# A graph network with four residual layers on one core: loads of the preamble in one queue, x^T with two tiles interleaved, and the last two batches as groups of one

## The chip, the cores and the metric

The kernel runs on one core of a Trainium2 chip, in fp32. The metric is the device time of one execution in microseconds, the median over several runs. TensorE (PE) has two rows in a profile: PE for the matmuls and PEld for the loads of the stationary operand. VectorE is DVE, ScalarE is ACT, GpSimd is POOL, SyncE is SP. A "q" behind a name (SPq, ACTq) is that engine's issuing of DMAs.

## The reference

x has 64 batches of 256 nodes by 128 channels; adj is 256 by 256 and shared by all batches. Four layers follow each other, each with a residual and a layer norm:

```python
# layer 0: x and three propagations by A (twice, the same A), one weight for each of the 7
x = layernorm(x + sum_k([x, A x, A^2 x, A^3 x, A x, A^2 x, A^3 x][k] @ W0[:, :, k]))
# layer 1
x = layernorm(x + A @ (x @ W1) + b1)
# layer 2, A normalised by the degrees of A + I
x = layernorm(x + (D (A + I) D x) @ W2.T + b2)
# layer 3: a gated unit, five steps; in_matrix and out_matrix are both A
h = x
for _ in range(5):
    m = A @ h;  av = concat([m, m]);  u3 = h @ U3.T + u3_b
    z = sigmoid(av @ W3.T + w3_b + u3);  r = sigmoid(av @ W4.T + w4_b + u3)
    hv = tanh(av @ W5.T + w5_b + (r * h) @ U5.T + u5_b)
    h = (1 - z) * h + z * hv
x = layernorm(x + h)
```

## The kernel before

The 64 batches are worked on in 32 groups of NB = 2. A group's tile is 128 partitions by 512: two batches of two tiles (T = 2) of 128 nodes, so Q = 4 tiles. Up to ACTIVE = 6 groups are in work at once. `Group.record` writes down all operations of one group; nothing is issued then.

A planner (`Plan.order`, line 75) afterwards sets the order of all instructions. Each operation has an engine, a cost, a lag to its consumers, a rank and the tiles it needs from slots (54 for work tiles, 8 PSUM banks, 9 for x, 16 in DRAM). The planner always places the operation that can start first on its engine; of several, the one of lowest rank. The rank of a group is its number; in the last LEVEL = 6 groups it is 26 plus a tenth per group plus a hundredth per operation already recorded, so that these groups advance side by side, each ten operations behind the one before. On the chip every engine follows that order, with semaphore waits, so a queue such as SP's is in order.

**Preamble** (lines 216 to 342). PE runs WARM = 24 transposes of the identity (`warmed`, line 226). adj is loaded (a_nat), transposed (p_at, aT), squared (p_a2, a2T). The weights of layer 0 (w0_raw) become four sums (w0s, line 263): the identity and W0[0], then W0[k] + W0[k+3] for k = 1 to 3. aTp (line 273) is A^T with its rows permuted, written by four SBUF-to-SBUF DMAs. `load` (line 210) takes the issuing engine: adj, w0_raw and the biases are issued by SP, nine other loads (w1s, b1s, six in `raw`, b2s) by ACT.

**Layer 0** (lines 519 to 561) needs x^T as the stationary operand. For the first HEAD = 2 groups PE transposes x (ptx). For the others DVE transposes 32 by 32 blocks (tx, line 469), SP writes the tile to DRAM (dx), and `brought` (line 474) reads it back with four DMAs, which puts the blocks in place. The node index of that x^T is interleaved over the four tiles: `by_node(xT)[:, q]` takes every fourth element, a step of 16 bytes. A^2 x is computed transposed (pmq, mq). `first` multiplies both by w0s into two PSUM banks, `moved` copies the half that A still has to be applied to (v), `second` applies it and adds it in PSUM, `summed` copies the result (s0). `statistics` and `normalise` are the layer norm: DVE's mean and variance (st, mv, ve), a power on POOL (rs), DVE's scaling (y).

**Layers 1 and 2** propagate (pm, m), multiply by the weight (py) and add y with the bias (yb, on POOL).

**The five steps** (lines 586 to 604) hold h transposed (hT): propagation (pmg, mg), products into pr and ph, the gates r, z and hv on ACT, and rh, d, e, hT on DVE. Between steps `packed` (line 486) brings hT back to node order: DVE's block transpose (th), one write to DRAM (dh), and one read per batch (h). That h has two tiles interleaved (`pair_of`, a step of 8 bytes), which the permuted aTp matches.

**The end.** The last END = 4 groups turn hT by PE (pth), the others by DVE and DRAM (tn, dn, hn). Then the residual, the layer norm, and one output DMA per group.

Line 190 is the helper `mm` that records every matmul, 404 the copies out of PSUM, 508 the gates, 515 DVE's two-operand instructions; groups of instructions are therefore told apart by their tiles.

Of the kernel before, what the change touches and what calls it, by code (L numbers as in the profile page):

```python
# [16 lines left out]
HEAD = 2  # L17
LEVEL = 6
END = 4
STEPS = 5  # L20
WARM = 24
# [4 lines left out]
class Val:  # L26
# [3 lines left out]
    def __init__(self, kind, shape, name):  # L30
        self.kind, self.shape, self.name = kind, shape, name
        self.writer, self.readers, self.users = None, [], []
        self.slot = self.ap = None
# [115 lines left out]
def kernel(  # L149
# [42 lines left out]
    SHAPES = {"bank": [P, 512], "x": [P, 512], "w": [P, 512], "dram": [P, 512], "st": [P, Q * 6], "mv": [P, Q * 2],  # L192
              "ve": [P, Q], "rs": [P, Q]}
    slots = {"bank": BANKS, "x": ACTIVE + 3, "w": 54, "dram": 16, "st": 8, "mv": 8, "ve": 8, "rs": 8}
# [3 lines left out]
    def constant(name, shape):  # L198
        v = Val("const", shape, name)
        v.ap = const.tile(shape, F32, name=name)  # L200
        return v
# [4 lines left out]
    def pre(rank, engine, cost, run, reads=(), writes=()):  # L206
        lag = {"SP": 2300, "ACTq": 2700, "PE": 260, "DVE": 260, "ACT": 130, "POOL": 100}[engine]
        plan.add(engine[:3] if engine == "ACTq" else engine, cost, lag, rank, run, reads, writes)

    def load(rank, engine, name, shape, src):  # L210
        v = constant(name, shape)
        queue = nc.sync if engine == "SP" else nc.scalar
        pre(rank, engine, 450, lambda: queue.dma_start(v.ap, src), [], [v])
        return v
# [18 lines left out]
    a_nat = load(-9, "SP", "a_nat", [P, T, N], adj.rearrange("(t p) m -> p t m", p=P))  # L233
# [13 lines left out]
    pre(-8, "DVE", dve_cost(512), lambda: nc.vector.tensor_copy(flat(aT), p_at.ap), [p_at], [aT])  # L247
# [11 lines left out]
    w0_raw = load(0, "SP", "w0_raw", [P, C, K0], w0)  # L259
# [8 lines left out]
    pre(-7, "DVE", 1300, w0_sums, [w0_raw], [w0s])  # L268

# [35 lines left out]


    w1s = load(0, "ACTq", "w1s", [P, C], w1)
    b1s = load(0.1, "ACTq", "b1s", [P, C], bass.AP(tensor=b1.tensor, offset=b1.offset, ap=[[0, P], [1, C]]))
    raw = {name: load(0.2, "ACTq", f"raw_{name}", [P, src.shape[1]], src)
           for name, src in (("w2", w2), ("w4", w4_w), ("w3", w3_w), ("w5", w5_w), ("u3", u3_w), ("u5", u5_w))}  # L310
    b2s = load(0.2, "ACTq", "b2s", [P, C], bass.AP(tensor=b2.tensor, offset=b2.offset, ap=[[0, P], [1, C]]))
# [33 lines left out]
    def view(ap, g):  # L345
        return ap[g * NB:(g + 1) * NB].rearrange("b (t p) c -> p (b t) c", p=P)

    def nat(v):
        return v.ap.rearrange("p (q c) -> p q c", q=Q)

    def parts(v):
        return v.ap.rearrange("p (t b c) -> p t b c", t=T, b=NB)

    def four(v):
        return v.ap.rearrange("p (b k c) -> p b k c", b=NB, k=2)

    def by_node(v):
        return v.ap.rearrange("p (n q) -> p q n", q=Q)
# [4 lines left out]
    def pair_of(v, q):  # L363
        return v.ap.rearrange("p (b c t) -> p b t c", b=NB, t=T)[:, q // T, q % T, :]

    def plain(v):
        return [v.ap[:, b * N:(b + 1) * N] for b in range(NB)]

    def by_block(v):
        o = v.ap.rearrange("p (k b t i) -> b p t k i", k=4, b=NB, t=T)  # L370
        return [o[b] for b in range(NB)]

    class Group:
        def __init__(self, g):
            self.g, self.first, self.last = g, None, None
            self.gate = self.load_gate = ()
            self.count = 0

        def val(self, kind, name):
            return Val(kind, SHAPES[kind], f"{name}_{self.g}")  # L380

        def add(self, engine, cost, lag, run, reads=(), writes=()):
            after = () if self.first else self.gate
            self.count += 1
            rank = self.g
            if self.g >= G - LEVEL:
                rank = G - LEVEL + (self.g - G + LEVEL) / 10 + self.count / 100
            op = plan.add(engine, cost, lag, rank, run, reads, writes, after)
# [7 lines left out]
        def dve(self, cost, run, reads, writes):  # L396
            return self.add("DVE", cost, 260, run, reads, writes)

        def act(self, run, reads, writes, cost=act_cost(512)):
            return self.add("ACT", cost, 130, run, reads, writes)  # L400
# [6 lines left out]
        def statistics(self, tag, s):  # L407
            st, mv, ve, rs = (self.val(k, k + tag) for k in ("st", "mv", "ve", "rs"))

            def stats():  # L410
                for q in range(Q):
                    nc.vector.bn_stats(st.ap[:, q * 6:(q + 1) * 6], nat(s)[:, q, :])  # L412

            def aggr():
                for q in range(Q):
# [4 lines left out]
            self.dve(775, stats, [s], [st])  # L420
            self.dve(410, aggr, [st], [mv, ve])
            self.add("POOL", 1010, 100,
                     lambda: nc.gpsimd.tensor_tensor(rs.ap, ve.ap, half, op=OP.pow), [ve], [rs])  # L423
            return mv, rs

        def residual(self, tag, ps, resid, left=lambda v: v.ap, right=lambda v: v.ap):
            s = self.val("w", "s" + tag)
            self.dve(dve_cost(512), lambda: nc.vector.tensor_add(right(s), left(ps), right(resid)),  # L428
                     [ps, resid], [s])
            return (s, *self.statistics(tag, s))  # L430

        def normalise(self, tag, s, mv, rs):
            y = self.val("w", "y" + tag)

            def run():
                for q in range(Q):
# [3 lines left out]
            self.dve(1030, run, [s, mv, rs], [y])  # L440
            return y

        def propagate(self, tag, h, aTs, ins=None, outs=None):
# [3 lines left out]
            def run():  # L447
                o, a = (outs or plain)(ps), ins or tile_of
                for b in range(NB):
# [3 lines left out]
            self.pe(pe_cost(N, NB * T), run, [h, aTs], [ps])  # L453
            return self.copied("m" + tag, ps)

        def transposes(self, tag, src):
            ps = self.val("bank", "pt" + tag)

            def run():
                for q in range(Q):  # L460
                    nc.tensor.transpose(ps.ap[:, q * P:(q + 1) * P], src.ap[:, q * P:(q + 1) * P], ident)  # L461

            self.pe(pe_cost(P, Q) / 2, run, [src], [ps])
            return ps

        def turned(self, name, src, ins, outs):

            t, far = self.val("w", "t" + name), self.val("dram", "d" + name)
            self.dve(dve_cost(512), lambda: nc.vector.transpose(t.ap.rearrange(outs, k=4, q=Q),
                                                                src.ap.rearrange(ins, k=4, q=Q)), [src], [t])  # L470
# [198 lines left out]
```

## Time and profile before

| | us |
|---|---|
| median of 3 runs | 1396.2 (1394.82 to 1396.5) |
| the profiled execution's own time | 1396.12 |
| its span, first to last instruction | 1394.3 |
| PE busy | 1374.0 (99% of the span) |
| DVE busy | 972.9 (70%) |
| ACT busy | 508.0 (36%) |
| POOL busy | 230.8 (17%) |
| mean granted TensorE clock | 0.994 |

A row of a group reads: line, engine, operation, output tile <- input tiles, shape, count, then busy time in us and the mean ns of one, then the idle time before them and what ended it. A row of a timeline begins with the start and the length in us; `x8` means that eight instructions are merged in it. An fp32 matmul appears as two MATMUL and two LDWEIGHTS instructions. A row of stretches has the stretch, its length, and the busy time of PE, PEld, DVE, ACT and POOL, then the granted clock, the DMA engines' share and GB/s.

### The profile page before, as it was taken

To read this page: it belongs to the slowest core of one execution; us is meant where nothing else is said; L and a number is where in the kernel's file an instruction comes from. 1 tells how busy PE (TensorE), PEld (TensorE's weight loads), DVE (VectorE), ACT (ScalarE), POOL (GpSimd) and SP (SyncE) were. 2 spreads that over 40 slices of the span, in tenths; PEclk is the share of its full clock that TensorE was granted. 3 is DMA by queue.
4 is the path that set the end of the run, shared out by engine and by line. 5 is a ranking of instruction groups with operands and counts; after the bars stand their busy time and mean duration, and the time that the engine had idled before them with its cause. 6 is when DMAs were issued, how large, how long until landed. Compare 5 with 4: busy or idle time off the path is not lost.

```text
span 1394.3 us, 16512 instructions
## 1 busy us (share of the span) xinstructions
PE 1374.0 (99%) x4998; PEld 926.1 (66%) x4998; DVE 972.9 (70%) x2701; ACT 508.0 (36%) x807; POOL 230.8 (17%) x199
## 2 busy tenths in 40 slices
PE   8999999999999999999999999999999999999995
PEld 7866667667666677666766666676666676765552
DVE  4756676767766777757767677775776778775575
ACT  2233433333334333443333333334334323334442
POOL 1401022202210131201202101111121122220000
PEclk9999999999999999999999999999999999999998
DMA  6022243324233332324323334233333232323231
GB/s 172 31 76 81 79 128 106 114 65 118 91 113 91 98 107 76 111 78 136 102 80 106 94 96 117 81 115 88 107 104 108 76 99 84 113 69 98 85 97 53
DMA packets 255049, 133.95 MB, mean 96 GB/s; under 512 B 146545, under 2 KB 226801, under 8 KB 254961
## 3 DMA queue, kind: packets, MB, share of 16 engines
q1 hardware_dynamic: 253664, 132.12, 32.2%
q8 instruction: 40, 0.66, 0.2%
q10 hardware_dynamic: 1296, 0.79, 0.2%
q14 instruction: 49, 0.39, 0.1%
HBM read 67.05 MB, written 65.54 MB: 95 GB/s over the span
## 4 chain that ended last, share of the span: by engine, by line
PE 95%; DVE 3%; issue 1%; DMA 1%; POOL 0%; ACT 0%; SPq 0%; POOLq 0%; DVEq 0%
PE pr L190 29%; PE pmg L190 19%; PE ph L190 19%; PE py L190 16%; PE pm L190 8%; PE pmq L190 4%; DVE y L437 1%; DMA x<-in_x_dram 1%; DVE st L412 1%; POOL rs L423 0%; DVE e L515 0%; DVE hT L515 0%; DVE s L428 0%; DVE d L515 0%; PE pth L461 0%
## 5 line engine op out<-in xcount | busy, mean ns | idle before, releaser
L190 PE MATMUL pr<-mg,w435u5T 128*128 128x512 f32 x640 | 321.0, 593 | 2.0 <-ACT mg L404 2.0
L423 POOL TENSOR_TENSOR rs<-ve,half 128x4 f32<-128x4 f32 x128 | 134.6, 1053 | 1063.4 <-DVE ve L417 1057.3
L515 DVE TENSOR_TENSOR d<-hv,hT 128x512 f32<-128x512 f32 x160 | 111.3, 696 | 190.2 <-ACT hv L508 189.8
L190 PE MATMUL pmg<-aTp,h 128*128 128x256 f32 x1024 | 241.7, 381 | 0.0
L190 PEld LDWEIGHTS pmg<-aTp,h 128*128 128x128 f32 x1024 | 201.3, 197 | 48.6 <-issue 23.3
L515 DVE TENSOR_TENSOR rh<-r,hT 128x512 f32<-128x512 f32 x160 | 115.0, 719 | 131.4 <-ACT r L508 130.0
L190 PEld LDWEIGHTS pr<-mg,w435u5T 128*128 128x128 f32 x640 | 119.9, 190 | 103.3 <-issue 93.0
L404 ACT COPY mg<-pmg 128x512 f32<-128x512 f32 x160 | 93.8, 586 | 237.0 <-PE pmg L190 223.3
L437 DVE TENSOR_SCALAR y<-s,mv,rs 128x128 f32<-128x128 f32 x512 | 146.9, 351 | 37.2 <-POOL rs L423 36.7
L508 ACT ACTIVATE z<-pr,bsum 128x512 f32<-128x512 f32 x160 | 110.0, 688 | 155.8 <-PE pr L190 141.8
L190 PE MATMUL ph<-rh,w435u5T 128*128 128x512 f32 x320 | 162.0, 593 | 0.3 <-DVE rh L515 0.3
L190 PE MATMUL ph<-mg,w435u5T 128*128 128x512 f32 x320 | 162.3, 592 | 0.0
L190 PE MATMUL pr<-hT,w2u3T 128*128 128x512 f32 x320 | 161.3, 593 | 0.4 <-DVE hT L515 0.4
L508 ACT ACTIVATE r<-pr,bsum 128x512 f32<-128x512 f32 x160 | 110.0, 688 | 136.2 <-PE pr L190 134.0
L508 ACT ACTIVATE hv<-ph,bsum 128x512 f32<-128x512 f32 x160 | 110.0, 687 | 53.8 <-PE ph L190 53.3
L515 DVE TENSOR_TENSOR e<-z,d 128x512 f32<-128x512 f32 x160 | 111.7, 702 | 2.5
L515 DVE TENSOR_TENSOR hT<-hT,e 128x512 f32<-128x512 f32 x160 | 109.3, 687 | 2.7
L412 DVE BATCH_NORM_STATS2 st<-s 128x6 f32<-128x128 f32 x512 | 109.4, 277 | 0.8
L190 PEld LDWEIGHTS ph<-rh,w435u5T 128*128 128x128 f32 x320 | 60.1, 190 | 71.6 <-issue 59.2
L190 PEld LDWEIGHTS ph<-mg,w435u5T 128*128 128x128 f32 x320 | 60.5, 190 | 69.5 <-issue 54.3
L190 PEld LDWEIGHTS pr<-hT,w2u3T 128*128 128x128 f32 x320 | 60.0, 190 | 50.4 <-issue 32.0
L490 DVE STREAM_TRANSPOSE th<-hT 128x512 f32<-128x512 f32 x128 | 90.2, 706 | 1.7
(77 smaller groups left out, 1412.9 us busy)
## 6 DMA issues: line engine op xcount, KB each, us to landing
dh<-th SPq DMA_DIRECT2D x160, 256.0 KB, 2.0
h<-dh SPq DMA_DIRECT2D x256, 128.0 KB, 2.5
x<-in_x_dram SPq DMA_DIRECT2D x32, 256.0 KB, 3.2
hT<-dh SPq DMA_DIRECT2D x128, 64.0 KB, 2.0
out_dram<-y SPq DMA_DIRECT2D x32, 256.0 KB, 2.4
dx<-tx SPq DMA_DIRECT2D x30, 256.0 KB, 2.2
xT<-dx SPq DMA_DIRECT2D x120, 64.0 KB, 2.0
dn<-tn SPq DMA_DIRECT2D x28, 256.0 KB, 2.0
```

Of the source, the lines that this page charges most:

```text
L190: nc.tensor.matmul(o, lhsT, rhs, start=start, stop=stop, skip_group_check=shared)
L404: self.act(lambda: nc.scalar.copy(t.ap, ps.ap), [ps], [t])
L412: nc.vector.bn_stats(st.ap[:, q * 6:(q + 1) * 6], nat(s)[:, q, :])
L423: lambda: nc.gpsimd.tensor_tensor(rs.ap, ve.ap, half, op=OP.pow), [ve], [rs])
L437: nc.vector.tensor_scalar(nat(y)[:, q, :], nat(s)[:, q, :], mv.ap[:, 2 * q:2 * q + 1], rs.ap[:, q:q + 1], op0=OP.subtract, op1=OP.mult)
L490: self.dve(dve_cost(512), lambda: nc.vector.transpose(turn.ap.rearrange("p (u j t) -> p u t j", t=T, j=32), src.ap.rearrange("p (u t i) -> ...
L508: self.act(lambda: nc.scalar.activation(t.ap, ps.ap, func, bias=bias[1], scale=1.0), [ps, bias[0]], [t], act_cost(512) + 100)
L515: self.dve(dve_cost(512), lambda: nc.vector.tensor_tensor(out(t), way(a), way(b), op=op), [a, b], [t])
```

## The change

It has three parts and the generalisation that they need.

- **Preamble.** `load` loses its engine: all loads are issued by SP, ordered by ranks that follow the need (a_nat -9; x of group 0 has 0; w0_raw 0.01; x of group 1 has 1; w1s 1.3, b1s 1.4, the others 1.5). WARM is 12. aT is copied out of PSUM by ACT, not DVE. The planner counts a lag of 4500 ns for the first x loads, 2700 for the others.
- **x^T.** For groups beyond HEAD (now counted in batches: 4) DVE's transpose writes with two tiles interleaved, and one DMA per batch reads the tile back from DRAM, with 256-byte pieces. Channels come out permuted: partition 4j + r holds channel 32r + j. A second copy of the first two weight sums, w0p, has its rows permuted to match; four SBUF-to-SBUF DMAs on SP make it.
- **Groups of one.** A group has its own nb, start and width; `ONES = (0, 2)` makes the last two batches groups of one, so that there are 31 groups of two and two of one. Their tiles use half of a slot. END is counted in batches (8). The gates that limit the groups in work count batches. x loads take the group's rank, which matters in the last region.

```diff
-WARM = 24
+WARM = 12
+ONES = (0, 2)
...
-    def load(rank, engine, name, shape, src):
+    def load(rank, name, shape, src):
         v = constant(name, shape)
-        queue = nc.sync if engine == "SP" else nc.scalar
-        pre(rank, engine, 450, lambda: queue.dma_start(v.ap, src), [], [v])
+        pre(rank, "SP", 450, lambda: nc.sync.dma_start(v.ap, src), [], [v])
...
-    pre(-8, "DVE", dve_cost(512), lambda: nc.vector.tensor_copy(flat(aT), p_at.ap), [p_at], [aT])
+    pre(-8, "ACT", act_cost(512), lambda: nc.scalar.copy(flat(aT), p_at.ap), [p_at], [aT])
...
-    w0_raw = load(0, "SP", "w0_raw", [P, C, K0], w0)
+    w0_raw = load(0.01, "w0_raw", [P, C, K0], w0)
...
+    w0p = constant("w0p", [P, 2, C])
+
+    def permuted():
+        for r in range(4):
+            nc.sync.dma_start(w0p.ap.rearrange("(j r) k c -> r j k c", r=4)[r], w0s.ap[32 * r:32 * (r + 1), 0:2, :])
+
+    pre(1.2, "SP", 1800, permuted, [w0s], [w0p])
...
+        def rank(self):
+            g = self.start / NB
+            return g if g < G - LEVEL else G - LEVEL + (g - G + LEVEL) / 10 + self.count / 100
...
-            plan.add("SP", 450, 2700, g, lambda: nc.sync.dma_start(nat(x_), view(x, g)), [], [x_],
+            plan.add("SP", 450, 4500 if self.start < HEAD else 2700, self.rank(), lambda: nc.sync.dma_start(nat(x_), self.view(x)), [], [x_],
                      self.load_gate)
 
-            if g < HEAD:
-                xT = self.copied("xT", self.transposes("x", x_))
+            near = self.start < HEAD
+            if near:
+                xT, w01 = self.copied("xT", self.transposes("x", x_)), w0s
             else:
 
-                xT = self.brought("xT", self.turned("x", x_, "p (q k j) -> p q k j", "p (k i q) -> p q k i"))
+                w01 = w0p
+                turn, far = self.val("w", "tx"), self.val("dram", "dx")
+                xT = self.val("w", "xT")
+                self.dve(lambda: nc.vector.transpose(
+                    turn.ap.rearrange("p (r b i t) -> p r b t i", r=4, t=T, i=32),
+                    x_.ap.rearrange("p (b t r j) -> p r b t j", r=4, t=T, j=32)), [x_], [turn])
+                self.add("SP", 420, 2000, lambda: nc.sync.dma_start(far.ap, turn.ap), [turn], [far])
+
+                def run():
+                    f = far.ap.rearrange("(k j) (r b n) -> b (j r) k n", k=4, r=4, b=self.nb)
+                    for b in range(self.nb):
+                        nc.sync.dma_start(xT.ap.rearrange("p (b k n) -> b p k n", b=self.nb, k=4)[b], f[b])
+
+                self.add("SP", 450 * self.nb, 2300, run, [far], [xT])
...
-                    for b in range(NB):
-                        o, n0 = p.ap[:, b * 2 * C:(b + 1) * 2 * C], b * N + t * P
-                        mm(o, xT.ap[:, n0:n0 + P] if g < HEAD else by_node(xT)[:, b * T + t, :], w0s.ap[:, 0:2, :], b == 0, True, shared=True)
-                        mm(o, qT.ap[:, n0:n0 + P], w0s.ap[:, 2:4, :], False, True, shared=True)
+                    for b in range(self.nb):
+                        o, q = p.ap[:, b * 2 * C:(b + 1) * 2 * C], b * T + t
+                        mm(o, (tile_of if near else pair_of)(xT, q), w01.ap[:, 0:2, :], b == 0, True, shared=True)
+                        mm(o, tile_of(qT, q), w0s.ap[:, 2:4, :], False, True, shared=True)
...
+    sizes = [1] * ONES[0] + [NB] * ((B - sum(ONES)) // NB) + [1] * ONES[1]
     groups = []
-    for g in range(G):
-        group = Group(g)
-        if g >= ACTIVE:
-            group.gate = (groups[g - ACTIVE].last,)
-        if g >= ACTIVE + 2:
-            group.load_gate = (groups[g - ACTIVE - 2].last,)
-        elif g >= HEAD:
-            group.load_gate = (groups[g - HEAD].first,)
+    for i, nb in enumerate(sizes):
+        group = Group(sum(sizes[:i]), nb)
+        end = group.start + nb
+        done = [o for o in groups if o.start + o.nb <= end - NB * ACTIVE]
+        loaded = [o for o in groups if o.start + o.nb <= end - NB * (ACTIVE + 2)]
+        if done:
+            group.gate = (done[-1].last,)
+        if loaded:
+            group.load_gate = (loaded[-1].last,)
+        elif group.start >= HEAD:
+            group.load_gate = (groups[i - 2].first,)
```

The rest of the diff replaces NB, Q and the fixed widths by the group's own, in shapes, loops and planner costs.

## The prediction, made before the change was run

> **What bounds the kernel now.** I read the page's busy shares first, then the busy time of three stretches, then the timelines of the two ends, then the groups by shape. Page:
>
> ```profile
> span 1394.3 us, 16512 instructions
> PE 1374.0 (99%) x4998; PEld 926.1 (66%) x4998; DVE 972.9 (70%) x2701; ACT 508.0 (36%) x807; POOL 230.8 (17%) x199
> PE   8999999999999999999999999999999999999995
> ```
>
> Stretches (PE busy is the third figure):
>
> ```profile
> 0.00:18.67 18.67, 14.73 (x70) 12.98 (x71) 7.69 (x21) 4.50 (x8) 1.42 (x7) 0.91 0.53 154
> 18.67:1355.00 1336.33, 1335.43 (x4861) 900.58 (x4860) 941.74 (x2609) 494.14 (x785) 225.34 (x188) 1.00 0.33 97
> 1355.00:1394.30 39.30, 23.80 (x69) 12.52 (x67) 23.49 (x74) 9.32 (x14) 4.03 (x4) 0.84 0.19 54
> ```
>
> PE idles 0.9 us in 1336: the middle is PE work laid end to end, and only less PE time per group shortens it. The ends are latency. The head, from chain, timeline and 2-us stretches (last three figures: granted clock, DMA share, GB/s):
>
> ```profile
> 1.36 5.19 PE L228 MATMUL warm<-ident 128*128 128x128 f32 x24 [1.36 <-POOL ident masks.py:199]
> 2.21 8.02 DMA x<-in_x_dram
> 11.39 2.61 PE p_a L190 x8
> 14.67 1.99 PE pmq L190 x8
> ...
> 8.00:10.00 2.00, 0.73 (x4) 0.42 (x4) 1.59 (x7) 0.00 (x0) 0.00 (x0) 0.91 0.62 184
> 10.00:12.00 2.00, 1.72 (x6) 1.58 (x7) 0.70 (x3) 0.89 (x2) 0.00 (x0) 0.50 0.36 81
> ```
>
> The adjacency lands at 3.73, but its transposes wait until 6.28 behind 24 warm-up transposes; then PE, in order, waits for x of groups 0 and 1 (landed at 9.2 and 10.2, 7.4 and 8.0 us after issue; the median of this load is 3.2), and squares A at a granted clock of 0.50. Dense work, from py of group 0, starts at 18.8.
>
> The tail:
>
> ```profile
> 1371.29 0.69 ACT L508 ACTIVATE hv<-ph,bsum 128x512 f32<-128x512 f32 x1 [0.17 <-PE ph L190]
> 1374.77 3.44 PE L190 MATMUL pmg<-aTp,h 128*128 128x256 f32 x8
> 1384.97 0.69 DVE L515 TENSOR_TENSOR hT<-hT,e 128x512 f32<-128x512 f32 x1
> 1390.14 1.12 DVE L437 TENSOR_SCALAR y<-s,mv,rs 128x128 f32<-128x128 f32 x4 [1.19 <-POOL rs L423]
> ```
>
> From 1374.7 one group of two batches goes down a chain that nothing fills, its pmg at half clock (3.44 where 1.89 is usual). By shape:
>
> ```profile
> L190 PE MATMUL py<-w0s,xT 128*128 128x256 f32 x256 | 80.8, 397 | 0.0
> L190 PE MATMUL py<-w0s,mq 128*128 128x256 f32 x256 | 76.1, 379 | 0.0
> L190 PEld LDWEIGHTS py<-w0s,xT 128*128 128x128 f32 x256 | 69.6, 309 | 9.3 <-issue 2.6 <-PE py L190 0.7 <-PE pr L190 0.5
> L190 PEld LDWEIGHTS pmg<-aTp,h 128*128 128x128 f32 x1024 | 201.3, 197 | 48.6 <-issue 23.3 <-PE ph L190 4.1 <-PE pr L190 2.6
> ```
>
> x^T with four tiles interleaved (16-byte steps) takes 309 ns to load as weights; h, with two interleaved, takes 197 and is hidden.
>
> **Part 1, x^T.** Eight py instructions (four on xT, four on mq) take 1.79 us at 32.27 and at 35.06, and 1.72 in group 0, where xT is contiguous: 0.07 per half group, 0.14 per group. The new layout has h's step, and pmg on h goes at the pace of pmg on y (241.7/1024 and 60.5/256, both 236 ns), so all of it goes: 30 groups' worth x 0.14 = **-4.2 us**, on PE's path in the packed middle. Beside it: DVE's transpose falls from 1110 ns (row tx) to about 706 (th), 12 us in all, costing nothing on a 70% DVE; SP issues two loads a group for four (60 issues fewer at 0.45-0.6), into twice as many 256-byte pieces, landing as h does in 2.5 us for 2.0. SP and DMA (share 0.33) are covered as long as xT arrives before PE reaches it. w0p adds four SP issues (part 2) and a wait of PE's: py of group 2 wants it, issued by about 11.6 and landed, at aTp's 3.4, by 15, far ahead of 26.
>
> **Part 2, the preamble.** All loads go to SP: a_nat, x0, w0_raw, x1, then nine that ACT issued (9 x 0.45 = 4.1 us of SP time), then aTp (four issues, 2.44 us before), w0p (four, taken the same, also bounded by h's 0.47 each: 1.9 to 2.4), x2, and the biases (six, 4.9 us before). SP thus reaches aTp near 6.7, x2 near 11.7 (11.97 before), dx of group 2 near 17 (17.69 before). The xT loads of group 2 then land near 22.5; PE needs them at 32.27 before, 26.4 after an advance of 5.9. So nothing is cost for SP's extra work, with some 4 us of cover; What stands behind w0p's wait for w0s in SP's queue is x2, the biases and dx2; w0s follows w0_raw (6.5 before) by some 1.5 us of DVE, so SP, there at 9.2, doesn't wait. aTp and the step weights are needed much later. ACT, freed, copies aT (586 ns by the a2T row, 692 on DVE).
>
> x0: 512 KB stand ahead of its end instead of most of the 1.8 MB moved by 10 us. At the 400 GB/s seen near 3 us it lands by 4.5; with the dip to 100 GB/s at 4.3-5.3, by 6. PE doesn't want it before 7.5. The Trainium skill (DMA: Bandwidth & Descriptors, "Issuing engines are not separate DMA queues") says queues share the same 16 DMA engines, so a second queue only saves issue time. Alone, that gives no gain here and 4.1 us more of SP; the row of 8.0 against 3.2 says order matters. I take the row; by the rule alone x0 would stay at 9.2 and the head gain fall to about 4.
>
> PE: 12 warm-ups at 0.21 end near 3.9; p_at four at half clock 0.86, to 4.8; aT copy to 5.4; p_a2; a2T copy; ptx0, ptx1 beside it; pmq0, pmq1 (1.73 each), p_an and the two weight transposes (1.1 together). If the clock rises at 6.2 as in this trace: p_a2 ends at 7.5, pmq0 starts at 8.4, dense work 8.4 + 3.45 + 1.1 = 12.95, a gain of 5.9. The clock is the doubt. The trace: warm-ups 206 ns apart (p_an's, at full clock: 140 to load), so half clock until about 6.2; falls at 9.6, rises at 13.0. The skill (TensorE: Matmul & The Clock Gate, "The HAM clock gate") wants about 3.4 us of sustained activity in a free-running window; 12 warm-ups give 2.6, and PE then idles 0.65 for aT. By the rule p_a2 may stay at half until 9.6: it ends at 8.9, dense work starts at 14.85, a gain of 4.0. The trace's window of 9.6-13.0 was about 89% busy and did raise the clock; the new one would be near 79%. I take between, leaning to the trace: **-5.3 us** (ends -2.5, with x late too, and -7).
>
> **Part 3, two groups of one.** Before, from 1355 PE has 20.7 us of work at full clock in 39.3: 18.6 lost. Of this 14.0 lie after the last pmg starts at 1374.66 (19.64 less 5.6 of work), the rest are waits of 0.67, 0.68 and 3.05 and small ones. With one batch the same chain is: pmg four at 0.215 and 0.17 to read, 1.03; copy 0.43; pr 0.6; r 0.47 (688 less 256 columns at 0.83); rh 0.42 (the 256-wide DVE copy: 411); ph 0.6; hv 0.47; d, e, hT 1.26; pth 0.35; s 0.42; st, mv, ve 0.85; rs 1.05; y 0.6; output 3.05 as before. Sum 11.6, with 3.3 of PE work: 8.3 lost. Before it stands the round trip of h (th, dh, h: 6.6 us before, about 5.9 with one load), filled by the other single, five operations ahead, and the last pair; I leave 2 us of gaps and 0.5 of half clock. Lost 10.8, a gain of 7.8. Costs: `second` streams 128 columns, 1.08 per batch by the py<-w1s row against 1.72 per pair, +0.45; more short DVE and ACT instructions and two more chains of POOL powers (1.05 each; POOL 17%) lie beside PE; seven groups stand open in the last region where six did, on 54 slots and 8 banks. No row shows that: from 0 (PE loses 0.9 us in the middle now) to the whole gain; I take 0, since singles hold a bank half as long. The new ranks of x loads only bring late x forward, at no cost with nine x slots. Net **-7.3 us** (-3 to -9.5).
>
> **Sum.** -4.2 - 5.3 - 7.3 = -16.8 on the profiled run's own 1396.12 (span 1394.3 and 1.8 around it), 0.1 from the median of 1396.2: **1379.3 us**. About 0.2% (2.8 us) is what a measurement of this kernel can tell from no change.
>
> **Rivals.**
> - *The head hardly pays* (0.16): half clock until 9.6 and PE empty near 25, as xT of group 2 comes late. For: SP has 13 issues ahead of everything. Against: freed ACT, the cover above. 4.2 + 7.3 + 1.5: about 1383.
> - *The tail hardly pays* (0.15): fixed latencies (rs 1.05, output 3.05, DMA round trips near 6) don't halve, and two singles in step wait at the same times, PE idling before each pmg. For: the 3.05 idle of before is just such a round trip. Gain 2 instead of 7.3: 1384.6; with the head at its low end of 2.5 as well, 1387.4.
> - *x^T stays slow, or PE's pace isn't set by those loads*: the change doing not what it says (0.03): 1383.5.
> - *Slower* (0.04): SP's single in-order queue becomes the bound at the start. If one of its waits (w0p on w0s, dx2 on DVE) holds x2, dx2 and xT behind it, PE has only groups 0 and 1 to work on. It decides once xT of group 2 lands later than 26.4 plus the gain, near 43; at 48 the run is 1401. Against: w0_raw stands third in the queue and landed at 6.5 even in the crowd.
>
> **How the numbers follow.** The forecast's own case has 0.62 and spans 1375 to 1383.5. The rivals of 1383 to 1387 have 0.34 together; a range of 1374 to 1387 leaves out the slower case, mixtures of two weak parts, and a tail or head better than both ends. Faster by over 0.2%: 0.94; within: 0.02; slower: 0.04.
>
> **What would show it.** py<-xT weight loads near 197 ns with matmuls at 379; tx near 0.7 us; x0 landed by 6 and py of group 0 starting near 13 (14.9: the clock rule was right); PE unbroken from there to some 20 us before the end; last pmg about 11.6 us before the end. Wrong: idle PE between 20 and 60 us or in the last 170, py of group 0 after 16, or a last pmg over 15 us before the end.

## The result, and the profile after

The changed kernel takes 1383.24 us (median of 6 runs, 1381.69 to 1384.2), the kernel before 1395.4 in the same comparison (6 runs, 1394.66 to 1396.5): a ratio of 0.9911 with a 95% interval of [0.9899, 0.9924], 12 us less. The profiled execution took 1382.45, with a span of 1380.7. A second set of runs of the same kernel gave 1381.79 (after2, below); the experiments are set against that one. The kernel before varies with its mean granted clock: over the 38 executions run beside the experiments its span goes from 1390.1 us at a clock of 0.998 to 1394.9 at 0.994, while the changed kernel's eleven lie between 1379.6 and 1382.4 at 0.997 or 0.998, so at a like clock the difference is nearer to 10 us than to 12.

The page's head, after. PE busy fell by 7.5 us; the last of the 40 slices went from 5 to 6 tenths, the first from 8 to 9.

```profile
span 1380.7 us, 16602 instructions
PE 1366.5 (99%) x5044; PEld 922.5 (67%) x5044; DVE 970.5 (70%) x2735; ACT 513.1 (37%) x833; POOL 236.1 (17%) x205
PE   9999999999999999999999999999999999999996
```

Three stretches (first the length, then the busy time of PE, PEld, DVE, ACT and POOL; last three figures: clock, DMA share, GB/s). The packed middle loses 1.0 us in 1325, as it lost 0.9 in 1336 before.

```profile
0.00:14.52 14.52, 12.48 (x54) 10.79 (x55) 5.33 (x17) 4.59 (x8) 1.42 (x7) 1.00 0.56 165
14.52:1340.00 1325.48, 1324.47 (x4880) 892.54 (x4879) 934.31 (x2620) 494.42 (x798) 229.90 (x193) 1.00 0.34 97
1340.00:1380.70 40.70, 29.55 (x113) 19.16 (x111) 30.85 (x99) 14.11 (x27) 4.83 (x6) 0.94 0.25 68
```

The groups by shape, after: the load of x^T as weights takes 196 ns where it took 309, the matmul 379 where it took 397 (means).

```profile
L195 PE MATMUL py<-w0p,xT 128*128 128x256 f32 x240 | 71.5, 379 | 0.0
L195 PEld LDWEIGHTS py<-w0p,xT 128*128 128x128 f32 x240 | 46.2, 196 | 14.8 <-issue 9.4 <-PE py L195 0.7 <-PE pr L195 0.5
```

The head, from PE's timeline. Names are shown without their numbers, so p_a is the squaring of A (p_a2 in the kernel and in the expectations). Read the second column: p_a takes 3.78 us, twice the 1.89 of pmq, which has as many instructions of the same shape. And the last line has no bracket: PE comes to pm of group 0, the first matmul of layer 1, without an idle gap.

```profile
5.71 3.78 PE L195 MATMUL p_a<-aT,a_nat 128*128 128x256 f32 x8 [0.68 <-ACT aT L251]
9.29 1.50 PE L475 MATMUL ptx<-ident,x 128*128 128x128 f32 x8
11.06 1.89 PE L195 MATMUL pmq<-a2T,x 128*128 128x256 f32 x8
27.26 1.89 PE L195 MATMUL pm<-aT,y 128*128 128x256 f32 x8
```

The same matmul in the kernel before:

```profile
30.76 1.89 PE L190 MATMUL pm<-aT,y 128*128 128x256 f32 x8
```

x of groups 0 and 1 lands 3.6 and 4.7 us after its issue, where it took 7.4 and 8.0.

The tail. The first four lines are PE's timeline, from the last batch's last pmg on; the others are DVE's in the same stretch, where instructions of three groups alternate (128x512 is pair 60, 128x256 are the batches 62 and 63). PE waits 2.64 us for an hT of DVE, and DVE has no gap over 0.6 us between 1367 and 1376.

```profile
1367.27 1.03 PE L195 MATMUL pmg<-aTp,h 128*128 128x256 f32 x4
1368.75 0.70 PE L195 MATMUL pr<-mg,w435u5T 128*128 128x256 f32 x2 [0.46 <-ACT mg L419]
1370.77 0.60 PE L195 MATMUL ph<-rh,w435u5T 128*128 128x256 f32 x2
1374.00 0.41 PE L475 MATMUL pth<-ident,hT 128*128 128x128 f32 x2 [2.64 <-DVE hT L529]
```

```profile
1369.80 0.42 DVE L529 TENSOR_TENSOR hT<-hT,e 128x256 f32<-128x256 f32 x1
1370.15 0.42 DVE L529 TENSOR_TENSOR rh<-r,hT 128x256 f32<-128x256 f32 x1
1370.67 1.11 DVE L451 TENSOR_SCALAR y<-s,mv,rs 128x128 f32<-128x128 f32 x4
1371.70 0.42 DVE L443 TENSOR_TENSOR s<-pth,y 128x256 f32<-128x256 f32 x1
1372.04 0.41 DVE L529 TENSOR_TENSOR d<-hv,hT 128x256 f32<-128x256 f32 x1
1372.37 0.48 DVE L427 BATCH_NORM_STATS2 st<-s 128x6 f32<-128x128 f32 x2
...
1377.08 0.60 DVE L451 TENSOR_SCALAR y<-s,mv,rs 128x128 f32<-128x128 f32 x2 [0.88 <-POOL rs L438]
```

By place: the matmuls on x^T give 4.5 us (busy time of their rows: 80.8 before; 71.5 and, for the first two groups, 4.8 after). Pm of group 0 starts at 27.26 for 30.76: 3.5 from the head. The rest of the 13.6 between the spans, about 5.6, is the tail's, with whatever the groups of one cost elsewhere; in after2, whose span is 1380.0, the same remainder is 6.3.

### The profile page after: what moved, and what is told of

Same layout as the page of the kernel before. It is cut to its first block, busy times and chain, and to the rows that moved or that the text cites. A ratio compares the mean times of both kernels' runs of the same rounds, so it can differ in the third digit from the quotient of the medians.

```text
span 1380.7 us, 16602 instructions
## 1 busy us (share of the span) xinstructions
PE 1366.5 (99%) x5044; PEld 922.5 (67%) x5044; DVE 970.5 (70%) x2735; ACT 513.1 (37%) x833; POOL 236.1 (17%) x205
## 4 chain that ended last, share of the span: by engine, by line
PE 97%; DVE 2%; DMA 0%; ACT 0%; issue 0%; POOL 0%; SPq 0%; POOLq 0%; DVEq 0%
PE pr L195 30%; PE ph L195 19%; PE pmg L195 19%; PE py L195 16%; PE pm L195 8%; PE pmq L195 4%; DVE y L451 1%; DMA h<-dh 0%; DVE st L427 0%; PE p_a L195 0%; PE warm L232 0%; DVE s L443 0%; DVE d L529 0%; DVE mv L431 0%; DVE e L529 0%
## 5 line engine op out<-in xcount | busy, mean ns | idle before, releaser
L195 PE MATMUL pr<-mg,w435u5T 128*128 128x512 f32 (+1 forms) x660 | 323.3, 580 | 1.7 <-ACT mg L419 1.4
L438 POOL TENSOR_TENSOR rs<-ve,half 128x4 f32<-128x4 f32 (+1 forms) x132 | 137.9, 1049 | 1049.8 <-DVE ve L432 1049.7
L529 DVE TENSOR_TENSOR d<-hv,hT 128x512 f32<-128x512 f32 (+1 forms) x165 | 113.6, 690 | 189.6 <-ACT hv L522 189.2
L529 DVE TENSOR_TENSOR rh<-r,hT 128x512 f32<-128x512 f32 (+1 forms) x165 | 116.5, 706 | 128.2 <-ACT r L522 126.9
L195 PE MATMUL pr<-hT,w2u3T 128*128 128x512 f32 (+1 forms) x330 | 163.1, 580 | 1.1 <-DVE hT L529 1.1
L522 ACT ACTIVATE z<-pr,bsum 128x512 f32<-128x512 f32 (+1 forms) x165 | 111.3, 674 | 142.2 <-PE pr L195 137.4
L195 PE MATMUL ph<-mg,w435u5T 128*128 128x512 f32 (+1 forms) x330 | 163.4, 579 | 0.0
L195 PE MATMUL ph<-rh,w435u5T 128*128 128x512 f32 (+1 forms) x330 | 163.0, 579 | 0.0
L529 DVE TENSOR_TENSOR e<-z,d 128x512 f32<-128x512 f32 (+1 forms) x165 | 113.8, 691 | 2.5
L529 DVE TENSOR_TENSOR hT<-hT,e 128x512 f32<-128x512 f32 (+1 forms) x165 | 113.1, 687 | 2.5
```

The lines of the kernel that those rows point to most:

```text
L195: nc.tensor.matmul(o, lhsT, rhs, start=start, stop=stop, skip_group_check=shared)
L438: lambda: nc.gpsimd.tensor_tensor(rs.ap, ve.ap, half[:, :self.q], op=OP.pow), [ve], [rs])
L522: self.act(lambda: nc.scalar.activation(t.ap, ps.ap, func, bias=bias[1], scale=1.0), [ps, bias[0]], [t], act_cost(self.width) + 100)
L529: self.dve(lambda: nc.vector.tensor_tensor(out(t), way(a), way(b), op=op), [a, b], [t])
```

## The experiments

Twelve runs follow, one of them the changed kernel again. Each ran beside the kernel before on the same chip, and the ratios are to it. Here x is late or early by the time from its issue to its landing, and "pm of group 0" is the first matmul of layer 1.

**Undoing the two parts that can be undone alone.**

```diff
 # ones00
-ONES = (0, 2)
+ONES = (0, 0)
 # oldxt
-                w01 = w0p
...
+                w01 = w0s
+                xT = self.brought("xT", self.turned("x", x_, "p (q k j) -> p q k j", "p (k i q) -> p q k i"))
```

> The changed kernel with the last two batches again as one group of two (ONES = (0, 0)); preamble and x^T stay new. If the singles are worth what is left of the profiled gain after the head (3.7) and x^T (4.3), 13.6 - 8.0 = 5.6, this run is 5 to 6 us slower than the changed kernel, near 1388.5, and its last pmg starts 18 to 20 us before the end. If the tail gained from the clock or the order and not from the width, the run is within 2 us of the changed kernel.

> The changed kernel with the old x^T (four tiles interleaved, four reads of 64 KB per group, weights w0s); w0p is still written, but nothing reads it. If the 16-byte step of the weight load is what cost PE 0.14 us per group, loads of py<-w0s,xT take about 309 ns again, matmuls 397, and the run is 4.0 to 4.7 us slower than the changed kernel, near 1387.5. If the PE's pace was not set by those loads, it is within 1 us.

ones00: 1387.48 (1385.6 to 1389.66), ratio 0.9957 [0.9945, 0.9969], 5.7 over after2. From the last pmg to the end its profiled execution takes 17.6 us where the changed kernel takes 13.4:

```profile
1366.23 1.90 PE L195 MATMUL pmg<-aTp,h 128*128 128x256 f32 x8
```

This last pmg ran at full clock, where the kernel before, in the same order and behind the same wait of 3.05 us, had taken 3.44. So of the 19.5 of before, 2.0 were half clock in the tail of that one execution and 4.2 the size of the group. The profiled execution is the fastest of ones00's six, whose spans go from 1383.8 at a mean clock of 0.998 to 1387.9 at 0.995. So 4.2 of the 5.7 is shown as the width of the group; that the rest is the clock is likely, but none of the longer executions was traced.

oldxt: 1386.47 (1386.33 to 1388.21), ratio 0.9946 [0.9935, 0.9958], 4.7 over after2. Its weight loads are slow again:

```profile
L195 PEld LDWEIGHTS py<-w0s,xT 128*128 128x128 f32 x256 | 69.2, 305 | 11.0 <-issue 4.1 <-PE pr L195 1.0 <-PE py L195 0.2
```

So x^T is worth what the changed kernel's own trace gave it (4.5), and the tail about as much (5.6). In both runs something else was seen that neither touches: p_a took 1.99 us and not 3.78, from the same start in ones00 and from 5.49 in oldxt, and PE then waited before pm of group 0. This is ones00:

```profile
5.71 1.99 PE L195 MATMUL p_a<-aT,a_nat 128*128 128x256 f32 x8 [0.68 <-ACT aT L251]
26.91 1.97 PE L195 MATMUL pm<-aT,y 128*128 128x256 f32 x8 [1.21 <-DVE y L451]
```

The head of ones00 is the changed kernel's, instruction by instruction, and p_a begins at 5.71 in both. So p_a's pace was not set by the head's order.

**PE's wait ahead of p_a, filled.** Four identity transposes fill PE's wait for aT.

```diff
 # fill4
+    def filled():
+        for i in range(FILL):
+            nc.tensor.transpose(warm.ap[:, (i % 4) * P:(i % 4 + 1) * P], ident, ident)
+
+    pre(-8, "PE", 700, filled, [p_at], [warm])
```

> The changed kernel with four more identity transposes on PE between p_at and p_a2, where PE waits 0.7 us for aT. If the idle gap (and so a window that is not busy enough) kept the clock at half through p_a2, the clock now rises near 6.2, p_a2 takes about 2.2 us instead of 3.8, py of group 0 starts near 13 instead of 14.5, and the run is 1 to 1.8 us faster, near 1381.7. If the clock's rise follows the start of the warm-up by a fixed time or the gap does not matter, p_a2 stays at 3.8 and nothing moves (within 0.3).

fill4: 1381.92 (4 runs, 1381.89 to 1382.13), ratio 0.9912 [0.9899, 0.9925]: no less than the changed kernel (0.9911 and 0.9916), though p_a took 1.99 us and py of group 0 started 1.9 us earlier. That the filling brought the clock isn't shown: p_a took 1.99 in unfilled kernels too, and 2.69 in s0first, which has the same filling. PE's line and DVE's timeline of fill4 show where the 1.9 went:

```profile
27.27 1.97 PE L196 MATMUL pm<-aT,y 128*128 128x256 f32 x8 [1.71 <-DVE y L457]
```

```profile
20.74 0.39 DVE L589 COPY s<-py 128x256 f32<-128x256 f32 x1
23.37 0.71 DVE L551 STREAM_TRANSPOSE tx<-x 128x512 f32<-128x512 f32 x1 [2.24 <-DMA x<-in_x_dram]
24.00 0.39 DVE L589 COPY s<-py 128x256 f32<-128x256 f32 x1
24.31 0.85 DVE L433 BATCH_NORM_STATS2 st<-s 128x6 f32<-128x128 f32 x4
...
26.78 1.12 DVE L457 TENSOR_SCALAR y<-s,mv,rs 128x128 f32<-128x128 f32 x4 [0.51 <-POOL rs L444]
```

DVE takes its instructions in order. Between the two copies of group 0's s0 stands the block transpose of a later group, whose x SP issued late (near 18 us in the changed kernel, behind everything else in its queue); it waits 2.24 us, and group 0's layer norm waits with it. Pm of group 0 starts at 27.27, 0.01 from the changed kernel's. The same came out in warm24, which undoes the shorter warm-up:

```diff
-WARM = 12
+WARM = 24
```

> The changed kernel with 24 warm-up transposes again in place of 12. Theory (the warm-up is beside the wait for adj and p_a2's clock decides nothing, as pm of group 0 waits for y): warm-up ends by 5.0, p_a2 starts at most 1.2 later than in the changed kernel if all 24 run at half clock and not later if they run at full clock, first pm of group 0 between 26.9 and 27.6, time within 0.7 of the changed kernel's 1381.8. Rival (a longer warm-up brings the full clock earlier and that is worth its 1.9 us): p_a2 at 2.0 us instead of 3.8, first pm of group 0 near 25.5, time about 1380. Rival (12 more transposes hold up p_at): p_at starts after 4.8 instead of 3.76, all later work 1 us later, time about 1382.8.

warm24: 1382.6 (4 runs, 1382.3 to 1382.89), ratio 0.9914 [0.99, 0.9928]. The warm-up held p_at up to 5.79, p_a started at 7.06 and ran in 1.99 us; PE waited 0.98 us for y and started pm of group 0 at 27.55. The theory's time (within 0.7) was missed by 0.1, and the rival's 1380 did not come. The other rival was right that p_at is held up, and near in time (1382.8); but pm of group 0 came only 0.3 later for it, and the intervals can't tell the cost from none.

**Clearing what stands ahead of group 0's layer norm**, in two ways: x of groups 2 and 3 earlier and the biases later (early12); then, on top of fill4, DVE's order itself (s0first).

```diff
 # early12
-    pre(2.5, "SP", 2200, biases, [], [braw])
+    pre(5.5, "SP", 2200, biases, [], [braw])
...
-        elif group.start >= HEAD:
+        elif group.start >= 2 * HEAD:
 # s0first, in Group.record of fill4
+                if self.start >= 2 * HEAD:
+                    self.gate = (*self.gate, held[0])
...
             y = self.normalise("0", s0, *self.statistics("0", s0))
+            if self.start == 0:
+                held.append(self.last)
+                plan.add("DVE", 150, 150, 0.4, lambda: nc.vector.tensor_add(bsum.ap, braw.ap[:, :3], braw.ap[:, 3:]),
+                         [braw], [bsum], (self.last,))
```

(early12 also ranks the x loads of groups 2 and 3 at 1.45 and 1.46.)

> The changed kernel with x of groups 2 and 3 loaded without a gate and ahead of the step weights in SP's queue, and the six bias loads moved behind (rank 5.5). If what sets the head is SP's one queue (x of groups 2 to 4 late, DVE holding its transposes in order ahead of the first layer norm's copy, and PE waiting for y), the copy s of group 0 comes right after `second`, y of group 0 lands near 23.5 to 24.5 instead of 26.5 and the run is 1 to 2.5 us faster than the changed kernel. If the head is set by the clock or by the norm's own latency, it is the same within 0.5.

> The changed kernel with fill4's four identity transposes ahead of p_a2, and with VectorE's order in the head altered: the stream transposes of groups 4 and later, and bsum, come only after y of group 0, so that nothing that waits for a late x or a late bias stands ahead of group 0's second s0 copy. Theory (group 0's first pm waits for y because VectorE takes its instructions in order, 1.71 us in fill4, 1.2 in early12): the first pm of group 0 starts near 25.6 with a wait under 0.3, no other wait of more than 0.5 follows before 45 us, and the time is 1.3 to 1.9 below the changed kernel's 1381.8: about 1380.2. Rival (the gain is given back again by something later, the xT of groups 4 and 6 above all, which are now loaded later): pm1 of group 0 at 25.6, but one or two new waits of PE of together 1.2 to 1.7 between 30 and 50 us; time 1381.5 to 1382. Rival (it is p_a2's clock alone that sets y): pm1 of group 0 still at 27.2; time 1381.9.

early12: 1382.16 (4 runs, 1380.87 to 1382.73), ratio 0.9916 [0.9902, 0.993]. The wait only moved: DVE stood 4.59 and 1.09 us before the transposes of the next groups and 0.53 before bsum, the s0 copies came at 23.57, and PE waited 1.22 before pm of group 0 at 27.20. s0first did clear it, and so shows that DVE's order was the cause of the wait: pm of group 0 starts at 25.92, with none.

```profile
25.92 1.89 PE L196 MATMUL pm<-aT,y 128*128 128x256 f32 x8
```

Yet it took 1381.68 (4 runs, 1381.07 to 1382.09), ratio 0.9907 [0.9894, 0.9921], which the changed kernel's 1381.79 can't be told from. The planner's order differs from there on; PE's waits between 1000 and 1340 us have one that the changed kernel lacks:

```profile
PE ph L196 <- DVE rh L535: 0.8, 1, 0.8
```

From pm of group 0 to the last pmg it needs 1340.7 us, after2 1339.3: the 1.4 of the head is given back, 0.8 of it in that one wait. The other 0.6 I could not place. The gains that were expected of early12 (1 to 2.5) and of s0first (1.3 to 1.9) both failed to come. The rival of a gain given back was right, but not in its place (30 to 50 us) or its cause (a late xT).

**The queue.** The nine loads go to ACT again, first with the aT copy left on ACT (actq), then with it on DVE as before (actq_dve), then also with the lag that the planner assumed for them before, 2.7 us (actq2; in the other two it was 0.13).

```diff
-    def load(rank, name, shape, src):
+    def load(rank, name, shape, src, engine="SP"):
...
+        plan.add(engine, 450, 2300 if engine == "SP" else 2700, rank, lambda: queue.dma_start(v.ap, src), [], [v])
...
-    pre(-8, "ACT", act_cost(512), lambda: nc.scalar.copy(flat(aT), p_at.ap), [p_at], [aT])
+    pre(-8, "DVE", dve_cost(512), lambda: nc.vector.tensor_copy(flat(aT), p_at.ap), [p_at], [aT])
```

> The changed kernel with the nine loads of w1s, b1s, raw and b2s issued by ACT again; the order on SP stays (a_nat, x0, w0_raw, x1). If sharing the DMA engines with a second queue is what made x land 7.4 to 8.0 us after issue, x0 or x1 lands after 7.5 again; PE asks for x only near 9 because of the slow p_a2, so the time moves by 0 to +1 us. If only the place behind w0_raw mattered, x0 lands by 5 and the time is the same within 0.3; aTp and w0p leave SP some 3 us earlier without any effect.

> As in the run with ACT issuing nine loads, but the copy of aT is DVE's again, as before the change, so it isn't caught behind ACT's blocked issue (there aT waited until 10.2). x0 and x1 should land 7 to 8 us after issue again, at 8.5 to 11. If that lateness is what one queue removes, py of group 0 starts 1 to 2.5 us later than in the changed kernel (15 to 16.5) and the time is 0 to 1.5 us longer; if PE has slack for late x (p_a2 runs first), py starts within 0.5 us and the time is the same.

> The changed kernel with the nine loads of w1s, b1s, the raw weights and b2s issued by ACT again as in the kernel before, the aT copy on VectorE, and the planner told the same lag for these loads as before (2.7 us). It parts the queue from the moved copy and from the order of the transposes, which actq and actq_dve mixed in. Theory (two queues put bytes beside x, and x comes later; the single queue is what brings x early): x0 and x1 land 6.5 to 8 us after their issue, PE waits 1.5 to 3 us for x of group 0 ahead of its transposes, first py near 16 to 17.5, and the time is 1 to 2.5 above the changed kernel's: 1382.8 to 1384.3. Rival (the order of the queue costs nothing, as y of group 0 is set by the late loads on SP, which are freed here): x2 and x3 are issued about 4 us earlier, y of group 0 is ready by 26, and the time is 1380.5 to 1381.8.

| | time, us | ratio to before | x lands after its issue | pm of group 0 |
|---|---|---|---|---|
| changed kernel (after2) | 1381.79 | 0.9916 [0.9903, 0.993] | 3.4 and 5.8 | 27.29 |
| actq | 1386.58 | 0.9947 [0.9935, 0.9958] | 7.3 and 8.7 | 32.51 |
| actq_dve | 1389.29 | 0.9965 [0.9953, 0.9978] | 6.5 to 7.9 | 33.30 |
| actq2 | 1385.99 | 0.9938 [0.9924, 0.9951] | 6.0 and 7.3 | 31.82 |

All three are slower than the changed kernel by 4.2 us or more: more than the head had gained. The expectations of actq (0 to 1) and actq_dve (0 to 1.5) missed by far; none of the three had ACT's wait. actq_dve is not a clean reading, since the false lag put two weight transposes ahead of p_a and PE waited 4.21 and 1.95 us there for raw weights; actq2 is cleaner. There the cause is less the late x (PE's transposes of x start at 8.22 with no wait) than ACT itself. ACT's own timeline in actq2:

```profile
2.29 6.53 ACTq L218 DMA_DIRECT2D raw_w<-in_L_gnn_w_w_dram  x3
8.87 1.10 ACTq L218 DMA_DIRECT2D raw_u<-in_L_gnn_u_w_dram  x2
10.01 0.45 ACTq L218 DMA_DIRECT2D b2s<-in_L_gnn_b_dram  x1
10.49 0.59 ACT L261 COPY a2T<-p_a 128x512 f32<-128x512 f32 x1 [8.26 <-DMA raw_w<-in_L_gnn_w_w_dram]
```

The second column of the first line is not issuing time: each of the three issues takes 0.33 to 0.45. It is a wait. A completion semaphore is a counter that a DMA raises when it has landed. The built program of actq2 hands eight of them to its DMAs in turn, whichever engine issues them, and has the issuing engine wait until the last user of the semaphore has landed. The third of the raw_w loads shares its semaphore with w_raw (the profile's name for w0_raw), 448 KB, and so ACT stands until w_raw has landed at 8.47, and the copy of A^2 behind it until 10.49, though PE had ended p_a at 8.4. The chain of waits of actq says it in one line each; there it is aT that stands behind the load, and PE waits 5.79 us for it:

```profile
1.74 8.06 DMA w_raw<-in_L_gnn_weight_dram
9.82 0.34 ACTq L218
10.19 0.59 ACT aT L252
10.83 2.50 PE p_a L195 x5
```

In the changed kernel such waits stop SP alone, for 0.6 us on w_raw and 0.4 on x, and no wait of PE follows from them. And y of group 0 is held in actq2 by the same DVE order as in fill4, later still:

```profile
28.25 0.71 DVE L546 STREAM_TRANSPOSE tx<-x 128x512 f32<-128x512 f32 x1 [3.59 <-DMA x<-in_x_dram]
28.89 0.83 DVE L428 BATCH_NORM_STATS2 st<-s 128x6 f32<-128x128 f32 x4
```

My theory for actq2 had the sign right and the size and place wrong (py of group 0 at 16.88, as it said, but through PE's waits of 1.27 for aT, 1.26 for ahat and 1.09 for a weight, not for x); the rival, that freeing SP would bring x of groups 2 and 3 sooner, fell: SP issued them at 16.16. It had waited 4.5 us, on x's semaphore, before its fifth issue. No run has a late x alone, so what the early x is worth by itself stays open.

**The same kernel again, and the tail.** noln leaves out the last layer norm of pair 60 and of batch 62; ypool keeps it and puts its final multiply on POOL.

```diff
 # noln
-            return (s, *self.statistics(tag, s))
+            return (s,) if tag == "3" and self.start in (60, 62) else (s, *self.statistics(tag, s))
 # ypool, in normalise
+            if tag == "3" and self.start in (60, 62):
...
+                self.add("POOL", 350 * self.q, 100, run_pool, [s, mv, rs], [y])
+                return y
```

> The changed kernel itself once more, to stand beside the other runs of this chip. The squaring of A (p_a2) took 3.8 us in its first profile and 2.0 in profiles of other versions with the same first 8 us, so the phase of the clock's window should be chance: p_a2 can take either 2.0 or 3.8 here. If py of group 0 starts near 12.8 (p_a2 fast), PE will wait 1.2 to 1.7 us for y of group 0 near 26 and the total stays within 0.5 us of the first runs; if the head's gain were set by the clock, a fast p_a2 would give a run 1.8 us faster.

> The changed kernel without the last layer norm of the last pair and of the first single (batches 60, 61 and 62 are written before that norm): 2.5 and 1.4 us of DVE work fewer in the last 15 us; the last single is whole. If DVE's in-order queue lengthens the last chain (13.4 us from the last pmg where 11.6 was worked out for a free DVE), the last pmg now starts 11.3 to 12 us before the end and the run is 1.3 to 2.5 us faster. If the chain's own latencies are longer than worked out, it gains under 0.5.

> The changed kernel with the normalising multiply (y) of the last layer norm of pair 60 and of batch 62 on GpSimd (POOL) instead of VectorE; all else as it is, so the whole result is computed. Theory (the last batch's chain waits in VectorE's queue behind the other groups' norms, 1.1 us by noln, of which the y of pair 60 and of 62, 1.11 and 0.59 us long in the changed kernel, are the larger part): from the last pmg to the end 12.5 to 13.0 instead of 13.4, time 0.3 to 0.8 below the changed kernel's 1381.8. Rival (POOL has no room: it also computes rs, 0.74 and 0.70 us, and the y of 60 and 62 hold up rs of 63): rs of 63 starts over 0.3 after its ve, last pmg to end 13.4 to 15, time 1381.8 to 1383.5.

after2: 1381.79 (1381.33 to 1383.34), ratio 0.9916 [0.9903, 0.993]; pm of group 0 at 27.29, 13.4 us from the last pmg to the end. noln: 1381.11 (1380.77 to 1381.43), ratio 0.991 [0.9896, 0.9923]; 12.3 from the last pmg to the end. DVE's queueing behind the other groups' norms is worth 1.1 us in the trace, 0.7 by the medians, where 1.3 to 2.5 had been expected. ypool could not have it: 1382.59 (1382.0 to 1382.81), ratio 0.9913 [0.9899, 0.9926], 13.6 from the last pmg to the end. POOL's timeline says why, and the rival had it: the four multiplies take 3.39 us there and 1.11 on DVE, and rs of the last batch (last line), whose ve started at 1375.25 and takes 0.17, starts at 1376.12, once POOL is free.

```profile
1370.41 3.39 POOL L457 TENSOR_SCALAR y<-s,mv,rs 128x128 f32<-128x128 f32 x4
1373.77 0.71 POOL L438 TENSOR_TENSOR rs<-ve,half 128x2 f32<-128x2 f32 x1
1374.59 1.57 POOL L457 TENSOR_SCALAR y<-s,mv,rs 128x128 f32<-128x128 f32 x2
1376.12 0.72 POOL L438 TENSOR_TENSOR rs<-ve,half 128x2 f32<-128x2 f32 x1
```

No version that computes everything beats the changed kernel by more than the runs spread: fill4, early12, warm24, s0first and ypool lie between 1381.68 and 1382.6.

## Why the prediction was right, and where its sizes were off

- **x^T: right in mechanism and size.** -4.2 forecast, -4.5 measured in PE's rows, 4.7 when undone. The loads are at h's pace, the transpose at 0.70 us, and xT's two longer loads cost nothing on SP.
- **The order of the loads: right as to x.** It landed at 4.9 and 7.0 (3.6 and 4.7 after issues at 1.24 and 2.28), and PE did not wait for it. The row was taken against the rule of "Issuing engines are not separate DMA queues" (the Trainium skill, DMA: Bandwidth & Descriptors), which left 4 us of head gain for a late x. On the rule's own point, that engines share the DMA hardware, nothing here speaks against it. What decides in actq2 is which engine stands in the wait for a semaphore: ACT, with copies that PE wants behind it.
- **The head: -5.3 forecast, -3.5 measured.** The step that failed is "dense work 12.95, a gain of 5.9", shaded to 5.3 for the clock: it took the start of py of group 0 for the whole gain. Two limits stand at nearly the same time. In the profiled execution p_a ran at half pace and py started at 14.7, the value that the prediction had worked out by the clock rule (14.85, a gain of 4.0). In ones00, oldxt, fill4, early12, warm24 and ypool p_a ran in 1.99 us, py started up to 2.1 earlier, and PE waited 1.0 to 1.7 us before pm of group 0, which starts between 26.9 and 27.6 in all of them. The cover was named for xT of group 2 alone; the wait that was missed is that for y of group 0, in DVE's order behind the transposes of x tiles that the single queue issues last. The first rival's "PE empty near 25" was that wait in place, with another cause. What the 3.5 consists of was not taken apart: in warm24, where p_a ran in 1.99 us, the longer warm-up cost 0.3 before pm of group 0, and the new order of PE's first operations, the early x and the freed ACT were not tried one by one.
- **The tail: -7.3 forecast, about -5.6 measured (6.3 in after2).** Two terms were mis-sized. The chain of one batch was 11.6 by the sum of its own latencies and is 13.4 in the trace. Of the 1.8, noln shows 1.1 to be DVE's queue: with two singles and a pair ending together, DVE is busy 1.82 to 1.93 of each 2 us from 1368 to 1374, and the last batch's d, e and hT take their turns. "More short DVE instructions lie beside PE" was the cost set to nothing that did cost. The remaining 0.7 was not taken apart. And the loss before was put too high: the 69 PE instructions from 1355 on, "20.7 us of work at full clock", are 21.8 us busy in ones00, which ran them at full clock, so 17.5 us were lost and not 18.6 (after the change 11.2, 40.70 less 29.55, for 10.8). The gaps and half clock that it allowed for ahead of the last chain, 2.5, were 1.6, which hid part of this. Of what was gained, 2.0 is half clock that the profiled execution of the kernel before had in its tail and ones00's had not; how often the changed kernel's tail meets it isn't shown.
- **Slot pressure and SP's queue: rightly at nothing.** The middle idles 1.0 us, as before, and no wait for xT appears. The slower rival found nothing to stand on; group 2's xT was issued from 21.3 on and took 2.8 to 3.9 us, and PE wanted it at 28.99; that was later than worked out (SP came to x of group 2 at 13.23 for 11.7), but still in time.

The sum: -4.5 - 3.5 - 5.6 for -4.2 - 5.3 - 7.3, 13.6 for 16.8. The measured 1383.24 is 3.9 above the forecast and inside the stated range, but only 0.3 inside the forecast's own case (up to 1383.5), and it is nearly the first rival's 1383. That the number fell on this side is in part luck; what parts the two is the traces, since the head paid 3.5 and not that rival's 1.5. That both ends paid about two thirds to three quarters is the forecast's mechanism with its sizes too large.

## What to carry to other kernels

An earlier start is worth only what reaches the next point where engines meet: follow it past the first instruction to the first wait of the layer behind, and look on every in-order engine for what stands ahead of that consumer and itself waits for a DMA. A load issued by a compute engine can stand in a wait for earlier DMAs and holds that engine's other work behind it, so look at the copies queued behind the issues, not at the length of an issue. Where groups end together, add up what the shared vector engine owes to all of them before summing the latencies of the last.

## What the runs showed of the hardware

- The pace of p_a was a matter of chance. Code that is the same up to there, starting at the same 5.71 us, ran it in 3.78 us in one execution and in 1.99 in another. Over the profiles of kernels with the changed kernel's instructions up to there (its own, after2, noln, ones00, oldxt, ypool) three were slow and three fast. The last pmg of before and of ones00, 3.44 and 1.90 us behind the same wait, shows the same in the tail. That fits the free-running window that the Trainium skill describes (TensorE: Matmul & The Clock Gate, "The HAM clock gate"): where the window's edge falls is not the kernel's. The window itself is in no trace here. I had leaned on one trace's edge at 6.2.
- The granted clock does not show the slow p_a. The stretches of the changed kernel say 1.00 from 6 to 10 us, while p_a's matmuls take 631 ns for 379 and its loads 332 for 190 (medians); in actq, where the rows from 10 to 14 us say 0.50, p_a takes the same 3.78. In these head stretches the pace of the instructions was the better clock.

```profile
6.00:8.00 2.00, 2.00 (x5) 1.54 (x5) 1.74 (x7) 0.00 (x0) 0.00 (x0) 1.00 0.98 316
8.00:10.00 2.00, 2.00 (x8) 1.60 (x7) 1.04 (x5) 0.47 (x1) 0.00 (x0) 1.00 0.42 109
```

- A load can wait for another that has no data in common with it. With eight semaphores in turn, the landing of an early transfer (w_raw's 448 KB, at 8.47 in actq2 and 9.80 in actq) decided when a later, smaller one (raw_w, 128 KB) was issued: at 8.5 and 9.82.
